# Attention's block-end visits two steps later, with their pieces on four PSUM tiles, and the sorting of tokens spread into single steps

## The chip, the cores and the metric

One core of one Trainium2 chip. The metric is the device time of one execution in microseconds (us), 1326.75 at the median of three runs of the kernel before. Engines are named as the profile names them: PE (TensorE), DVE (VectorE), ACT (ScalarE), POOL (GpSimd), SP (SyncE, which here issues most DMAs).

## The reference

The input is `x` of shape (2, 256, 56, 56): B = 2 images, C = 256 channels, N = 56·56 = 3136 tokens each. Cut to what is computed:

```
h   = non-local conv block(x)                 # gram matrices, 1x1 convs, batch norm, residual
t   = layernorm(tokens of h)                  # (2, 3136, 256)
t   = t + causal_attention(t, 4 heads of 64) @ W_proj
u   = layernorm(t)
p   = softmax(u @ W_gate)                     # 8 experts
top-2 experts per token, with their weights
t   = t + sum over its 2 experts of  w_e * (gelu(u @ W1[e] + b1[e]) @ W2[e] + b2[e])
out = t as (2, 256, 56, 56)
```

## The kernel before

**Stages.** The conv block takes the first 100 us or so. Attention goes to about 867 us, and the experts from there to the end. Within attention, token work of other kinds is fed in: the projections of the next stretch of tokens, the output projection of blocks that are finished, and the sorting of tokens by expert.

**Attention** (`attend`, L684 on). For each image b, each query block i of W = 448 tokens (7 of them) and each head pair hp (2) the kernel goes over the key tiles j of 128 tokens. All steps (i, hp, j) are written out into one list. A step has two halves. `scores` makes the products of keys and queries (L721) in a PSUM tile with the tag "sc" (two buffers), ACT takes their exponential (L729), DVE masks the tiles that the diagonal cuts (L731) and adds the rows up in `acc` (L739, L743). `values(n - 3)`, three steps later, multiplies with the values (L761) into the PSUM tile yp, of which there is one. After the last key tile ACT copies yp (L772) to `both`, and POOL adds its halves into `qT` (L773).

**Block ends.** When the scores of a block's last key tile are written, `visit(i, hp)` (L1966) and `sum_rows` (L776) follow on the spot. A visit runs the pieces that `ahead` (L1928) names: projections to query and key (qk, L603), to value (v, L618) or transposes (xp, L589) of the next stretch of tokens; two steps of the queue (`pull`); and two steps of the output projection (`products`, pp, L671). A piece makes some matmuls in a PSUM tile that `bank` (L522) gives from a pool of two, and ACT (L595, L611, L627) or DVE (L676) empties it. `sum_rows` sums `acc` over partitions (sp, L785); the sums go through DRAM (L790 to L796), `invert` (L805) takes the reciprocal, it goes out and comes back broadcast (L806, L811), and `scale` (L817) applies it to the block.

**The queue.** `tokens(b)` is a generator in a queue: `project_out` (L671: products, DVE sum, the statistics of the layernorm at L177 and L178), then `dispatch` (L1004: reciprocal root by Newton steps at L1040 to L1053, softmax, top 2, ranks by expert), then the scatter of token rows into expert order (`x_slots`, L1355 to L1363: DVE makes a row tile xr, POOL issues two indirect DMAs for each of 25 chunks of 128 tokens), and for b = 0 the loads of W1 (w1s, L1845) and of the experts' first rows. Each `yield` ends a step. `pull(n)` takes n steps. `between` (L1977), called once in every step of attention, pulls two steps at every second call.

**Experts** (L1380 to L1661). Some 102 blocks of 128 rows: the hidden layer ht (L1485), gelu (L1494), the transposes of a later block's inputs (tp, L1462), a copy of a later block's weights by DVE (w_f, L1473), the output yp (L1504), its bias (ys, L1514) and its store (y_slots, L1519, on SP). Blocks 0 to 41 are image 0's. Image 1's queue goes on beside them: `meanwhile` pulls two steps a block, three while image 1 is being sorted. The rows come in groups of three blocks. Group 14 (blocks 42 on) is the first with rows of image 1; it is fetched (L1403) at block 36, and ahead of that `need(1)` pulls the queue until all scatters of image 1 are issued. When the group has landed, DVE tests it (eq, L1428), adds two parts of its mixed rows (L1439), and goes on to the weights of block 41. A check of the softmax sums, `judge` (L1784 to L1789), ends in a small matmul, gdp (L1793).

**What sets the order.** In attention and in the experts the order on every engine is the order in which the program is written (`manual_schedule`), so the lists, the yields and the pulls above decide where an instruction stands on its engine.

Of the kernel before, what the change touches and what calls it, by code (L numbers as in the profile page):

```python
# [10 lines left out]
F32 = mybir.dt.float32  # L11
# [17 lines left out]
def conv_attn_moe_kernel(  # L29
# [52 lines left out]
    P = 128  # L82
# [429 lines left out]
    def layer1(nm, general):  # L512

        with ExitStack() as whole:
# [4 lines left out]
            bg = pool(whole, "bg", bufs=2)  # L519
            g1 = pool(whole, "g1", bufs=1)  # L520

            def bank(name, shape=(P, 512)):  # L522
                return pm.tile(list(shape), F32, tag="m", name=f"{name}_{nm}")

            def centre_gate(place):
# [135 lines left out]
            def project_out(b, qT, done):  # L661

                for first, m, k in pairs():
                    while done() < (first + m - 1) * P + k:
                        yield False
                    yield "pe"
                    for n in range(first, first + m):
                        o = n * P
                        ps = bank(f"pp_{b}_{n}")
                        for c in range(NH):  # L670
                            nc.tensor.matmul(  # L671
                                ps[:k, : C + E], qT[:, c, o : o + k], wpr[:, c, :],
                                start=(c == 0), stop=(c == NH - 1),
                            )
                        t = ts[b][:k, n, : C + E]
                        nc.vector.tensor_tensor(t, t, ps[:k, : C + E], ALU.add)  # L676
                        if b == 0:
                            nc.sync.dma_start(out=rest_d[:k, n], in_=t[:, :C])
                    stats(b, first, m, k, bg, f"o{nm}{b}")

                    for _ in range(3 if b else 1):
                        yield True

            def attend(  # L684
                b, qT, kT, v, fst, fs, psc, py, visit, between, clock, later, finished
# [62 lines left out]
                def values(n):  # L748
                    i, hp, j, first, last, order = steps[n]
                    k = chunk(j)  # L750
                    c0 = max(0, j * P - i * W)
                    sn = f"{nm}{b}_{hp}_{i}"
                    st = sts.pop(n)
                    if first:
                        yps[hp, i] = py.tile([P, 2, 512], F32, tag="y", name=f"yp_{sn}")
                    yp = yps[hp, i]

                    for h in range(0, k, HS):
                        end = last or (h and all(chunk(o) <= h for o in order[order.index(j) + 1 :]))
                        for a in range(2):  # L760
                            nc.tensor.matmul(  # L761
                                yp[a * HS : (a + 1) * HS, h // HS, c0:W],
                                v[hp][h : h + HS, j, a, :HS],
                                st[h : h + HS, a, c0:],
                                start=first,
                                stop=bool(end),
                            )
                    if last:

                        yh = qT[:, hp, i * W : (i + 1) * W]  # L770
                        both = fs.tile([P, 2, W], F32, tag="acc", name=f"both_{sn}")
                        nc.scalar.copy(both, yp[:, :, :W])  # L772
                        nc.gpsimd.tensor_tensor(yh, both[:, 0], both[:, 1], ALU.add)  # L773
                        del yps[hp, i]

                def sum_rows(hp, i):  # L776
                    yh = qT[:, hp, i * W : (i + 1) * W]
                    r = (b * NH + hp) * NB + i
                    sn = f"{nm}{b}_{hp}_{i}"
                    acc = accs.pop((hp, i))  # L780
                    sp = bank(f"sp_{b}_{hp}_{i}")

                    flat = acc.rearrange("p a w -> p (a w)")
                    for g in range(4):
                        nc.tensor.matmul(  # L785
                            sp[g * 32 : (g + 1) * 32, : W // 2], ones[:, :32],
                            flat[:, g * W // 2 : (g + 1) * W // 2], start=True, stop=True,
                        )
                    line = fs.tile([P, W], F32, tag="rb", bufs=3, name=f"line_{sn}")
                    nc.scalar.copy(line[:, : W // 2], sp[:, : W // 2])  # L790
                    halves = sum_d[r].rearrange("a (h w) -> (a h) w", h=2)
                    for g in range(4):
                        nc.sync.dma_start(
                            out=halves[g : g + 1], in_=line[g * 32 : g * 32 + 1, : W // 2]
                        )
                    nc.sync.dma_start(  # L796
                        out=sums[:, r], in_=sum_d[r].rearrange("a (p f) -> (a p) f", p=HS)
                    )
                    later.append((clock[0] + 4, invert, hp, i, yh))
# [27 lines left out]
                        later.sort(key=lambda e: e[0])  # L827

                ends = {i: max(n for n, s in enumerate(steps) if s[0] == i) for i in range(NB)}
                LAG = 3  # L830
                for n in range(len(steps) + LAG):
                    if 0 < n <= len(steps) and steps[n - 1][4]:
                        i, hp = steps[n - 1][:2]
                        visit(i, hp)
                        sum_rows(hp, i)
                    if n < len(steps):
                        i = steps[n][0]
                        between(i, ends[i] - n)

                    late = n >= LAG and steps[n - LAG][3]  # L840
                    if n >= LAG:
                        due(clock[0])
                        clock[0] += 1
                    if n >= LAG and not late:
                        values(n - LAG)
                    if n < len(steps):
                        scores(n)
                    if late:
                        values(n - LAG)
# [154 lines left out]
            def dispatch(b):  # L1004

                t = ts[b]
                tail = chunk(NCH - 1)
                ops = [0]

                def small_piece():  # L1010

                    if b:
                        yield True
# [5 lines left out]

                def op():  # L1020

                    ops[0] += 1
                    for _ in range(0 if b else 1 + ops[0] % 2):
                        yield True

                def small(name, last=E, dt=F32):
# [2 lines left out]
                def wide(ap):  # L1029
# [8 lines left out]
                    small(k, 1).rearrange("p t o -> p (t o)") for k in ("newton_x", "newton_y", "red")  # L1038
                )
                nc.vector.tensor_scalar(x, var, 1e-5, None, ALU.add)  # L1040
                nc.vector.tensor_scalar(
                    y.bitcast(I32), x.bitcast(I32), 1, None, ALU.arith_shift_right
                )
                nc.vector.tensor_scalar(
                    y.bitcast(I32), y.bitcast(I32), -1.0, float(0x5F3759DF), ALU.mult, ALU.add
                )
                yield from small_piece()
                for i in range(4):
                    to = var if i == 3 else y
                    nc.vector.tensor_tensor(z, y, y, ALU.mult)  # L1050
                    nc.vector.tensor_tensor(z, z, x, ALU.mult)
                    nc.vector.tensor_scalar(z, z, -0.5, 1.5, ALU.mult, ALU.add)
                    nc.vector.tensor_tensor(to, y, z, ALU.mult)  # L1053
                    yield from op()
                    yield from small_piece()
# [294 lines left out]
                for n in range(NCH):  # L1350
# [23 lines left out]
                        if b or k:  # L1374
                            yield True
                    if b == 0:
                        yield False
                sent[b] = True

            def experts(w1s, w2s, b2s, ex, es, ps6, between, need, written, settle, decide):  # L1380
# [538 lines left out]
            else:  # L1919
                fst = pool(att, "fst", bufs=5)  # L1920
                fs = pool(end, "fs", bufs=2, side="right")
                psc = pool(att, "psc", bufs=2, space=PSUM)
                py = pool(att, "py", bufs=1, space=PSUM)
                projections = [project_qkv(b, qT, kT, v, px) for b in range(B)]
                finished = [[0] * NH for b in range(B)]
# [37 lines left out]
                for b in range(B):  # L1963
                    queue.append(tokens(b, qT, lambda b=b: min(finished[b])))

                    def visit(i, hp):  # L1966

                        now, then = ahead(b, i, hp)
                        for piece in now:
                            piece()  # L1970
                        for _ in range(2):
                            pull()
                            products()
                        for piece in then:
                            piece()

                    def between(i, left):  # L1977
                        if b == B - 1 and i == NB - 1:

                            now = load_w2(left < NCH - 4)  # L1980
                            for _ in range(1 if left > NCH - 4 else 2):
                                next(now, None)

                        tick[0] += 1
                        if tick[0] % 2:
                            pull(2)

                    due = attend(
                        b, qT, kT, v, fst, fs, psc, py, visit, between,
# [252 lines left out]
```

## Time and profile before

| | us |
|---|---|
| runs | 1324.08, 1326.75, 1327.43 |
| the profiled execution | 1320.51 |
| its span, first to last instruction | 1318.7 |
| PE busy (96% of the span) | 1269.1 |
| DVE busy (61%) | 798.3 |
| ACT busy (46%) | 610.9 |
| POOL busy (26%) | 348.8 |
| a full step of attention (L721 and L761) | 1.50 |
| a block of the experts | 3.73 |
| scatters of image 1 on POOL | 958.66 to 1035.81 |

The mean granted clock of PE is 0.991. A row of the timeline reads: start, duration, engine, line, operation, output <- inputs, shapes, count, and in brackets the idle time of the engine just ahead of it with what ended it. In the view of waits a row names the instruction that waited, what it waited for, the sum in us, how often, and the longest. "issue" is time in which an engine waited for nothing that the profile shows.

### The profile page before, as it was taken

How to read it: one execution, taken by the hardware profiler on the slowest of the kernel's cores; microseconds unless marked ns; L12 is line 12 of the kernel's file. 1: busy time of each engine (PE TensorE's matmuls, PEld its weight loads, DVE VectorE, ACT ScalarE, POOL GpSimd, SP SyncE). 2: the span in 40 equal slices, each digit the busy share in tenths (PEclk: the TensorE clock that was granted, in tenths of full speed). 3: DMA queues.
4: the chain of work that ended last, by engine and by line, in shares of the span. 5: the costliest groups of instructions: out<-in, count | busy, mean ns of one | idle time of the engine just before them, and what ended most of it. 6: DMA issues, size and time to landing. Idle time of an engine off the chain costs nothing.

```text
span 1318.7 us, 28564 instructions
## 1 busy us (share of the span) xinstructions
PE 1269.1 (96%) x10809; PEld 827.2 (63%) x10809; DVE 798.3 (61%) x1673; ACT 610.9 (46%) x1235; POOL 348.8 (26%) x319
## 2 busy tenths in 40 slices
PE   9999999999999999999999999999998999899997
PEld 8875445544444555444444444579987899799996
DVE  1673566666777745756877777754753443355554
ACT  0255555556566544555655455633432333344432
POOL 1113330000002223311126620000066312665551
PEclk9999999999999999999999999999999899999999
DMA  9994100000000001000002243321234343466654
GB/s 317 359 349 129 31 16 24 25 17 16 17 9 8 25 1 37 18 11 9 16 24 81 81 133 95 105 72 53 69 128 147 117 113 94 139 195 193 189 162 132
DMA packets 111074, 123.88 MB, mean 94 GB/s; under 512 B 19703, under 2 KB 100840, under 8 KB 110930
## 3 DMA queue, kind: packets, MB, share of 16 engines
q1 hardware_dynamic: 100130, 95.18, 23.7%
q0 software_dynamic: 9840, 25.67, 5.7%
q8 instruction: 89, 1.46, 0.5%
q10 hardware_dynamic: 960, 1.11, 0.3%
q14 instruction: 55, 0.45, 0.1%
HBM read 62.06 MB, written 61.05 MB: 93 GB/s over the span
## 4 chain that ended last, share of the span: by engine, by line
PE 87%; DVE 6%; ACT 3%; issue 3%; DMA 1%; POOL 0%; SPq 0%; DVEq 0%; ACTq 0%; POOLq 0%
PE sc_f L721 18%; PE yp_f L761 18%; PE ht_f L1485 14%; PE yp_f L1504 13%; PE qk_f L603 7%; PE v_f L618 3%; PE cp L410 3%; DVE acc_f L743 2%; PE gram L317 2%; PE pp_f L671 2%; ACT st_f L729 2%; PE tp_f L1462 2%; PE sp_f L785 1%; PE yo_f L1727 1%; DMA out_dram<-ot_f 1%
## 5 line engine op out<-in xcount | busy, mean ns | idle before, releaser
L729 ACT ACTIVATE st_f<-sc_f 128x896 f32<-128x896 f32 (+5 forms) x400 | 330.4, 840 | 225.0 <-PE sc_f L721 199.3
L743 DVE TENSOR_TENSOR acc_f<-acc_f,st_f 128x896 f32<-128x896 f32 (+5 forms) x372 | 379.9, 1021 | 74.0 <-ACT st_f L729 62.2
L721 PE MATMUL sc_f<-qT_f,kT_f 64*64 64x448 f32 (+6 forms) x3184 | 340.6, 500 | 9.4 <-ACT st_f L729 6.0
L761 PE MATMUL yp_f<-st_f,v_f 64*64 64x448 f32 (+6 forms) x3184 | 339.9, 501 | 3.5 <-DVE st_f L731 2.3
L1494 ACT ACTIVATE g_f<-ht_f,b1b 128x128 f32<-128x128 f32 x408 | 116.5, 370 | 252.0 <-PE ht_f L1485 125.1
L721 PEld LDWEIGHTS sc_f<-qT_f,kT_f 64*64 64x64 f32 x3184 | 121.0, 133 | 164.5 <-issue 124.2
L761 PEld LDWEIGHTS yp_f<-st_f,v_f 64*64 64x64 f32 x3184 | 120.0, 133 | 154.3 <-issue 131.7
L1485 PE MATMUL ht_f<-xT_f,w_f 128*128 128x128 f32 x1632 | 206.4, 280 | 4.5 <-issue 3.6
L1485 PEld LDWEIGHTS ht_f<-xT_f,w_f 128*128 128x128 f32 x1632 | 201.7, 196 | 11.3 <-issue 6.0
L773 POOL TENSOR_TENSOR qT_f<-both_f 128x448 f32<-128x448 f32 x28 | 37.0, 1321 | 503.0 <-ACT both_f L772 503.0
L1363 POOL DMA_INDIRECT x_slots<-xr_f,idx x100 | 110.0, 1100 | 144.0 <-DVE xr_f L1361 100.8
L1473 DVE COPY w_f<-w1s_f 128x1024 f32 x102 | 72.7, 714 | 84.8 <-PE ht_f L1485 37.7
L574 POOL TENSOR_SCALAR xn_f<-t 128x256 f32<-128x256 f32 (+1 forms) x50 | 80.8, 1624 | 155.3 <-PE xp_f L589 66.2
L1525 POOL DMA_INDIRECT y_tokens<-ys_f,to_f x57 | 59.0, 1036 | 126.1 <-DVE ys_f L1514 102.3
L1514 DVE TENSOR_TENSOR ys_f<-yp_f,kT_f 128x128 f32<-128x128 f32 x102 | 29.5, 289 | 102.8 <-PE yp_f L1504 72.8
L603 PE MATMUL qk_f<-px_f,wat 128*128 128x512 f32 (+2 forms) x224 | 88.5, 547 | 0.8 <-ACT px_f L595 0.6
L603 PEld LDWEIGHTS qk_f<-px_f,wat 128*128 128x128 f32 x224 | 40.5, 190 | 46.2 <-issue 41.1
L739 DVE COPY acc_f<-st_f 128x896 f32<-128x896 f32 x28 | 17.9, 641 | 80.1 <-ACT st_f L729 76.3
L1504 PE MATMUL yp_f<-v_f,g_f 128*128 x204 | 62.2, 385 | 2.0 <-issue 1.9
L731 DVE TENSOR_TENSOR st_f<-st_f,keep 128x256 f32<-128x256 f32 (+1 forms) x112 | 45.6, 407 | 30.4 <-ACT st_f L729 29.8
L1504 PE MATMUL yp_f<-px_f,g_f 128*128 x204 | 62.3, 385 | 1.4 <-issue 1.4
L1504 PE MATMUL yp_f<-kT_f,g_f 128*128 x204 | 61.9, 384 | 1.1 <-issue 1.0
(285 smaller groups left out, 1268.4 us busy)
## 6 DMA issues: line engine op xcount, KB each, us to landing
x_slots<-fill SPq DMA_DIRECT2D x1, 8190.0 KB
xb_f<-x_slots SPq DMA_DIRECT2D x60, 130.0 KB
x_slots<-fill SPq DMA_DIRECT2D x1, 7296.0 KB
y_slots<-ys_f SPq DMA_DIRECT2D x57, 128.0 KB
kept<-t SPq DMA_DIRECT2D x2, 3200.0 KB
x<-in_x_dram SPq DMA_DIRECT2D x14, 448.0 KB
rb_f<-inverses SPq DMA_DIRECT2D x56, 112.0 KB
y_f<-y_tokens SPq DMA_DIRECT2D x23, 256.0 KB
```

Source lines behind the costliest of these rows:

```text
L574: nc.gpsimd.tensor_scalar(xn[:k, a], ts[b][:k, n + a, :C], ts[b][:k, n + a, MEAN : MEAN + 1], ts[b][:k, n + a, RSTD : RSTD + 1], ALU.subtr ...
L603: nc.tensor.matmul(ps[:, :w], wat[:, c, d0 : d0 + P], px[:, s % 2, c, :w], start=(c == 0), stop=(c == NH - 1),)
L721: nc.tensor.matmul(ps[h : h + HS, a, c0:W], kT[hp][rows, j * P + h : j * P + h + HS], qT[rows, hp, q0 + c0 : q0 + W], start=True, stop=True,)
L729: nc.scalar.activation(st[:k, :, c0:], ps[:k, :, c0:W], AF.Exp, scale=SCALE)
L743: nc.vector.tensor_tensor(acc[:k, :, c0:], acc[:k, :, c0:], st[:k, :, c0:], ALU.add)
L761: nc.tensor.matmul(yp[a * HS : (a + 1) * HS, h // HS, c0:W], v[hp][h : h + HS, j, a, :HS], st[h : h + HS, a, c0:], start=first, stop=bool( ...
L1363: s = nc.gpsimd.indirect_dma_start(out=xds[b], out_offset=bass.IndirectOffsetOnAxis(ap=idxs[b][:kk, k, n : n + 1], axis=0), in_=xr[:kk], i ...
L1473: nc.vector.tensor_copy(w, w1s[:, :, bass.ds(e, 1), :].rearrange("p c e h -> p c (e h)"))
L1485: nc.tensor.matmul(ht[:, k, :], w[:, c, k * P : (k + 1) * P], xT[:, c, :], start=(c == 0), stop=(c == NH - 1),)
L1494: nc.scalar.activation(g[:, k, :], ht[:, k, :], AF.Gelu, bias=b1bs[b][:, k, i : i + 1])
L1504: nc.tensor.matmul(yp[:, :C], g[:, k, :], w2s[k][:, bass.ds(e, 1), :].rearrange("p e d -> p (e d)"), start=(k == 0), stop=(k == KH - 1),)
L1525: s = nc.gpsimd.indirect_dma_start(out=y_tokens, out_offset=bass.IndirectOffsetOnAxis(ap=to[:, n % GB : n % GB + 1], axis=0), in_=ys, in_o ...
```

## The change

It has these parts. (1) A visit comes when the scores of two steps of the next block are written (`BEHIND = 2`), and `sum_rows` with it. (2) In a visit the pieces take in turn two tiles of the pool "m" and two of the scores' pool (`ring`). (3) `both` no longer has a buffer of its own and uses `acc`'s. (4) For image 0 the statistics after the output projection become a later piece per chunk (`closer`), put at the head of the queue, and three yields follow for either image. (5) In image 0's dispatch each operation, Newton's too, is a step of one yield; one yield was no step (`False`) behind its scatter and becomes one. (6) Visits pull no longer; `between` pulls one step at each call, but for the cut tiles of block 0. (7) W2's loads in the last block start a little later.

```diff
             def bank(name, shape=(P, 512)):
+                turn = ring[0] % 4 if ring else 0
+                if turn > 1:
+                    ring[0] += 1
+                    flat = score_banks[0].tile([P, 2, 512], F32, tag="sc", name=f"{name}_{nm}")[:, 0]
...
+                    return flat[:, : shape[1]]
+                if ring:
+                    ring[0] += 1
                 return pm.tile(list(shape), F32, tag="m", name=f"{name}_{nm}")
...
+                    if b == 0:
+                        queue.appendleft(closer(b, first, m, k))
+                        continue
                     stats(b, first, m, k, bg, f"o{nm}{b}")
 
-                    for _ in range(3 if b else 1):
+                    for _ in range(3):
                         yield True
+                while b == 0 and unclosed[0]:
+                    yield False
+
+            unclosed = [NCH]
+
+            def closer(b, first, m, k):
+
+                for n in range(first, first + m):
+                    stats(b, n, 1, k, bg, f"o{nm}{b}")
+                    unclosed[0] -= 1
+                    yield True
...
-                        both = fs.tile([P, 2, W], F32, tag="acc", name=f"both_{sn}")
+                        both = accs.pop((hp, i))
...
-                    acc = accs.pop((hp, i))
+                    acc = accs[hp, i]
...
-                LAG = 3
+                LAG, BEHIND = 3, 2
                 for n in range(len(steps) + LAG):
-                    if 0 < n <= len(steps) and steps[n - 1][4]:
-                        i, hp = steps[n - 1][:2]
+                    if BEHIND < n <= len(steps) + BEHIND and steps[n - 1 - BEHIND][4]:
+                        i, hp = steps[n - 1 - BEHIND][:2]
                         visit(i, hp)
                         sum_rows(hp, i)
                     if n < len(steps):
                         i = steps[n][0]
-                        between(i, ends[i] - n)
+                        between(i, ends[i] - n, (steps[n][2] + 1) * P > i * W + 1)
...
-                    ops[0] += 1
-                    for _ in range(0 if b else 1 + ops[0] % 2):
+                    if b == 0:
                         yield True
...
                     if b == 0:
-                        yield False
+                        yield True
                 sent[b] = True
...
                         now, then = ahead(b, i, hp)
+                        ring.append(0)
                         for piece in now:
                             piece()
                         for _ in range(2):
-                            pull()
                             products()
                         for piece in then:
                             piece()
-
-                    def between(i, left):
-                        if b == B - 1 and i == NB - 1:
+                        ring.clear()
+
+                    def between(i, left, cut):
+                        if b == B - 1 and i == NB - 1 and left < NH * NCH - 2:
...
                         tick[0] += 1
-                        if tick[0] % 2:
-                            pull(2)
+                        if not cut or i:
+                            pull()
```

In the order of the built programs, the rows of PE are the same in kind and number. The visits stand two steps later; the scatters of image 0 end 10 to 14 steps later; the output projection of image 1 has six chunks more behind attention; its ranks, keys and scatters stand five blocks of the experts later (its first row tile behind w_27, before behind w_22). At block 36, nine chunks of the scatter are left where there were two. From block 41 on the orders are the same.

## The prediction

> **What bounds the kernel now.** I read the busy shares first, then the costliest groups, then what TensorE (PE) waits for, and only then the stretches of time in which it waits.
>
> ```profile
> span 1318.7 us, 28564 instructions
> PE 1269.1 (96%) x10809; PEld 827.2 (63%) x10809; DVE 798.3 (61%) x1673; ACT 610.9 (46%) x1235; POOL 348.8 (26%) x319
> L721 PE MATMUL sc_f<-qT_f,kT_f 64*64 64x448 f32 (+6 forms) x3184 | 340.6, 500 | 9.4 <-ACT st_f L729 6.0
> ```
>
> PE is busy 96% of the span, so only 1318.7 - 1269.1 = 49.6 us are to be had at all without fewer matmuls. The order of instructions in the two programs shows the same 7387 rows on PE, so the change removes no matmul: it can only remove idle time of PE or add some. The view of what PE waits for says what the idle time is:
>
> ```profile
> PE sc_f L721 <- ACT st_f L729: 6.0, 9, 1.2
> PE yp_f L1504 <- issue: 4.2, 7, 1.0
> PE ht_f L1485 <- issue: 3.6, 8, 1.1
> ...
> PE gdp_f L1793 <- DVE judge_f L1789: 2.3, 1, 2.3
> PE yp_f L761 <- DVE st_f L731: 2.3, 4, 1.0
> PE xp_f L589 <- DVE t L676: 2.2, 6, 1.1
> ...
> PE sp_f L785 <- ACT kT_f L611: 1.8, 7, 0.3
> PE sp_f L785 <- DVE t L676: 1.1, 2, 0.6
> ```
>
> (us in total, times, longest.) Waits of the visits (xp L589, sp L785, qk, pp) are many and small. The timeline of one visit shows their form:
>
> ```profile
> 286.67 5.43 PE L603 MATMUL qk_f<-px_f,wat 128*128 128x384 f32 x16
> 291.93 3.72 PE L671 MATMUL pp_f<-wpr,qT_f 128*128 128x264 f32 x16
> 295.88 0.41 PE L589 MATMUL xp_f<-ident,xn_f 128*128 128x128 f32 x2 [0.23 <-DVE t L676]
> 296.22 0.58 PE L785 MATMUL sp_f<-acc_f,ones 128*32 128x224 f32 x8
> ```
>
> A visit of 10 us loses 0.23 us here. So the visits are long but full, and the second half of the profile, where the stall per occurrence is microseconds, weighs as much as they do.
>
> **Part 1: visits later, pieces on four tiles.** No instruction is added. Each gap of PE of 0.16 us or more between 104 and 866 us sums to about 19 us; by kind: sp, thirteen of 0.17 to 0.35 us, 3.2; xp 2.2 (one alone 1.15); pp 0.6; qk 0.2. These 6.2 us are waits for one of two tiles to be emptied, and four tiles give two more pieces (about 1.8 us by the pp row, 0.93 us each) of cover, so I count them gone. The two sp waits of 0.57 at 824.84 and 863.30 us come in the last block's visits, where few pieces rotate: they stay. Of the other gaps, yp<-DVE mask L731 (2.3 us, in four places) ends when two further steps of scores lie between a mask and its use: 0 to 2.3. The scatter zone of batch 0 (698 to 771 us: sc<-ACT exp 4.9, issue 2.0) sees its scatters spread over more steps and 10 to 14 steps later: 0 to 3. Against it: yp of the next block waits for ACT's copy L772 where the block is short (0.45 us in two places now, rows of i=0): with a visit's evacuations in ACT's queue ahead of the exps, 0 to 0.9 more. What hides the later sum chain (sums DMA, invert, inverses DMA, rb DMA: 3.8 + 4.2 + 3.7 us) is the next block, tens of us; its cover is gone only at the last block. Sum: -4 to -11 us, taken -7.5, near the 6.2 whose rows are plain plus something of the rest.
>
> A rule that speaks against it: the Trainium skill, "TensorE: Matmul & The Clock Gate", section "A second HAM failure mode: psum-queue depth-cycling", says that cycling through PSUM banks can leave micro-gaps that make the clock drop and recover over and over. The window rows here grant 1.00 in every stretch of attention while two tiles already turn; so by the row it costs nothing, by the rule the visits would run partly at half clock. I take the row.
>
> **Part 2: the end of attention.** At the change to the experts, sums go 864.3 to 870.4, inverses to 874.9, rb to 879.1, and DVE stands behind that chain: PE waits 1.48 us for a pp tile at 880.29 and 0.78 at 867.02. The last visit now comes after more of the closing values (L761), so the chain begins about 1.1 us later against the end of attention, and fewer pieces (pp of batch 1, six tiles of 0.89 = 5.3 us) remain done before it; that is work moved, not added. Cost 0 to +2.5, taken +1.5.
>
> **Part 3: batch 1's sorting comes later.** Visits no longer pull the queue, variances are pieces of their own, and every sorting step waits a turn. In the instruction order of the changed program the rank of batch 1 moves from before block 18 of the experts to before block 23, its first scatter row from after w_22 to after w_27: five blocks, at 3.73 us a block 18.7 us. The scatters must all be issued before the load of group 14, which the order puts at block 36 in both programs. Before, 2 chunks of 25 are left there; after, 9 (16 to 24), written in a row between w_37 and w_38. POOL's rows price them:
>
> ```profile
> 1038.55 0.19 PE L1793 MATMUL gdp_f<-ones,judge_f 128*1 128x1 f32 x2 [2.33 <-DVE judge_f L1789]
> 1038.66 3.44 PE L1485 MATMUL ht_f<-xT_f,w_f 128*128 128x128 f32 x16
> ...
> 1051.60 1.95 PE L1485 MATMUL ht_f<-xT_f,w_f 128*128 128x128 f32 x16
> ```
>
> ```profile
> 958.66 0.99 POOL L1363 DMA_INDIRECT x_slots<-xr_f,idx  x1 [90.54 <-DVE xr_f L1361]
> ...
> 989.49 0.97 POOL L1363 DMA_INDIRECT x_slots<-xr_f,idx  x1 [0.30 <-issue]
> ```
>
> One scatter is 0.97 + 0.30 us, a chunk two of them, 2.56; 25 chunks cannot take less than 64 us, and took 77.15 (958.66 to 1035.81). Now let S be 958.66. Before, block 36 starts at S + 69.7, POOL ends at S + 77.2, group 14 is issued on SP at 1037.51, lands and meets its test on DVE (eq L1428) at 1044.74 without a wait, and block 41 (ht at 1051.60) is S + 92.9: the load has several us to spare. After, the scatters start near block 27, S + 18.7. Nine more blocks at the rate that blocks 22 to 36 had under scatters (68.8 us for 14, 4.92 each) put block 36 at S + 63. Then 9 x 2.56 = 23 us, and some 2.6 us that POOL is behind by then (one chunk): POOL ends at S + 88.6. Then 1.7 us to SP's issue, 6 to the landing, 0.5 for eq and to, 0.96 for the sum L1439, 0.69 for the copy w_41 L1473, which stands behind them on DVE: block 41 starts near S + 98.4. Behind SP's waiting load stand y_slots of blocks 33 to 35, whose buffers (three) DVE needs again at block 36's rows; that stands behind w_41 too and ends with the same landing. So block 41 comes 5 us later. PE, done with block 40 at S + 82, stands idle some 14 us there; the stalls of 14.7 us "issue" that it has under scatters now (969 to 974, 999 to 1003, 1016 to 1021 us) are fewer, which is already in the 5.
>
> The clock adds to it. After 2.33 us of idle the row at 1038.66 shows 3.44 us for the 16 matmuls that take 1.95 in the row at 1051.60, and the window 1020 to 1040 a clock of 0.84. A longer idle should cost some 2.5 us (one slow ht, 1.5, and the slow yp behind it). The Trainium skill, the same page, "What's actually happening", gives half rate after an idle window of about 3.4 us and full rate after as long a busy one; by that the price would be about 1.7 us, as an estimate, and our 2.33 us of idle would not always be enough, while the row shows that it was.
>
> Bounds: if POOL has nothing left over and half of the 14.7 us of stalls go, block 41 is no later than now (0); if none of them go and they fall beside the burst, +14. Taken +7.5 (5 and 2.5).
>
> A gain I exclude: nothing is taken from PE or POOL in this part, and even at POOL's floor the scatters end at S + 18.7 + 64 = S + 82.7, after the S + 77.2 of before.
>
> **Spaced sorting of batch 0** (Newton steps one by one, the second scatter as a step): DVE does the same work, in more places. Its cover is attention; it ends about 14 steps (some 20 us) later, still before block (1,0,6), and the first rows for the experts are loaded behind it; w1s (8 loads) go beside w2's on SP. They still come 60 us ahead of the experts, so nothing. If that cover were gone: the first block would wait for the loads of early rows, some 6 us by the landing above.
>
> **Sum.** -7.5 + 1.5 + 7.5 = +1.5 us against the profiled execution, 1320.51 us (span 1318.7 and 1.8 around it): 1322.0. The median of the runs shown, 1326.75, lies 6.2 above it (their spread is 1324.08 to 1327.43), so I predict 1328.3.
>
> **Rivals.**
> - As forecast, gain and loss cancel: 1325 to 1331. Chance 0.36.
> - Faster: attention gives all (-9 to -11), and the wait at block 41 is hidden, since the stalls under scatters that go are as long as it (0 to +2): 1317 to 1322. For it: 14.7 us of such stalls exist. Against: the burst is written in the order, and POOL's rate has no slack in its rows. Chance 0.28.
> - Slower: the burst of nine chunks alone sets the time of block 41, and none of the stalls under scatters pay for it. It decides once POOL ends more than 13 us after block 36 starts (now 7.5; by my working 25). Its price is the upper bound, +12 to +14, with attention's and the turn's terms as above: -7.5 + 1.5 + 13 = +7 on 1326.75, so 1334, and 1331 to 1338 with the spread of attention's term. For it: POOL's rows have no slack in them, and the load has no second way. Chance 0.34.
> - It does not do what it says: visits wait as before, now for exps of the two steps ahead (sc tiles are shared with the scores). Then the 6.2 us stay, and the loss stays too: near 1335. Chance 0.02, and it counts with slower.
>
> A measurement of this kernel tells about 0.3%, 4 us, from no change. From these cases: faster 0.28, same 0.36, slower 0.36. The range, which leaves about 0.1 out at each end: 1317 to 1337.
>
> **What would show it.** In the profile after: the waits of xp, sp and qk in visits down to about 1 us together; the first scatter of batch 1 some 13 us after that of before (18.7, less what is gained ahead of it), nine chunks back to back on POOL, ending over 20 us after the start of block 36; DVE's eq L1428 with a wait for the xb DMA of some 10 us, and an idle stretch of PE of 10 us or more before block 41 with a clock of 0.8 or less in that window. I am wrong if that stretch is not there (then faster), or if the waits of the visits are (then slower).

## The result, and the profile after

The changed kernel takes 1330.74 us at the median of 13 runs (1326.35 to 1337.03), the kernel before 1326.28 in as many beside it: a ratio of 1.0044, 95% interval 1.0029 to 1.0058. That is slower by some 0.4%, just over the 0.3% that the prediction called no change, and inside its range. The profiled execution took 1329.87 us against 1320.51, 9.4 more; the medians differ by 4.5, since the profiled execution of before lies under all 13 of its runs. So the losses in the table below, read off these two profiles, are some 5 us larger in sum than those of the medians.

The page of the changed kernel, and what PE waits for (us in total, times, longest):

```profile
span 1328.2 us, 28525 instructions
PE 1268.9 (96%) x10809; PEld 824.0 (62%) x10809; DVE 785.1 (59%) x1673; ACT 612.8 (46%) x1235; POOL 345.9 (26%) x319
```

```profile
PE ht_f L1514 <- issue: 12.9, 19, 1.6
PE yp_f L1533 <- issue: 10.6, 11, 2.2
PE sc_f L746 <- ACT st_f L754: 5.1, 7, 1.9
...
PE sp_f L810 <- DVE t L687: 0.6, 1, 0.6
...
PE gdp_f L1822 <- DVE judge_f L1818: 0.5, 1, 0.5
```

The waits of the visits have nearly gone, as forecast: xp is no longer in the list, qk keeps its 0.6 us, and sp 1.6 us of its 4.4 (2.2 us together, where about 1 was forecast). What has grown is "issue" in the experts, from 7.8 to 23.5 us on ht and yp. The same visit as was shown of before, in the timeline:

```profile
284.19 5.43 PE L614 MATMUL qk_f<-px_f,wat 128*128 128x384 f32 x16
289.45 3.72 PE L682 MATMUL pp_f<-wpr,qT_f 128*128 128x264 f32 x16
293.01 0.38 PE L600 MATMUL xp_f<-ident,xn_f 128*128 128x128 f32 x2
293.32 0.59 PE L810 MATMUL sp_f<-acc_f,ones 128*32 128x224 f32 x8
```

From the first pp to sp it takes 3.87 us where it took 4.29. The bracket of before showed 0.23 us of idle there, but 0.42 us went: the row of pp is 3.72 long, and the next instruction can start 3.56 after it began. A bracket begins at the modelled end of the row before it, so the wait here is some 0.16 us longer than it says.

Where the time went, by the starts of the experts' blocks (us from the span's start, read off the ht rows of both timelines):

| | before | after | after less before |
|---|---|---|---|
| block 21 (the projections moved out of attention are done) | 955.8 | 942.2 | -13.6 |
| block 36 (group 14 is fetched) | 1028.3 | 1009.9 | -18.4 |
| block 41 (needs group 14 on DVE's way) | 1051.6 | 1057.1 | +5.5 |
| end of the span | 1318.7 | 1328.2 | +9.5 |

At block 21 the ranks of image 1 (about 1 us of PE) are done in before and still to come in after, so some 12.6 of the 13.6 us are gain. So attention gave about twice what was forecast, five blocks took back 23.9 us, and the rest 4.0; of these 2.3 are in waits of yo for DVE (3.3 us, before 1.0), and what the others are is not shown. In the five blocks PE did not stand at block 41, as the prediction had it. It crawled. The timeline, PE, then POOL at the same time:

```profile
1022.36 0.56 PE L1514 MATMUL ht_f<-xT_f,w_f 128*128 128x128 f32 x1 [0.38 <-issue]
1024.50 0.37 PE L1514 MATMUL ht_f<-xT_f,w_f 128*128 128x128 f32 x1 [1.57 <-issue]
1025.93 0.37 PE L1514 MATMUL ht_f<-xT_f,w_f 128*128 128x128 f32 x1 [1.06 <-issue]
...
1043.74 0.19 PE L1822 MATMUL gdp_f<-ones,judge_f 128*1 128x1 f32 x2 [0.54 <-DVE judge_f L1818]
1043.86 3.78 PE L1514 MATMUL ht_f<-xT_f,w_f 128*128 128x128 f32 x16
```

```profile
1036.99 0.91 POOL L1392 DMA_INDIRECT x_slots<-xr_f,idx  x1 [0.30 <-issue]
1038.21 0.91 POOL L1392 DMA_INDIRECT x_slots<-xr_f,idx  x1 [0.30 <-issue]
```

One matmul, at times two or three, in 0.7 to 2.8 us, from 1014 us on, for as long as POOL issues the scatters of the burst without a break, and some 4 us more. Block 37 takes 30.1 us. In before there are three such stretches, of 4 to 5 us (from 969, 999 and 1015 us). Behind the crawl one block is slow (block 38, 5.7 us), then PE goes at its full rate, and the rows of group 14 are not waited for: DVE tests them as soon as it has done what stands ahead of the test (no bracket), and blocks 40 and 41 start 3.73 us apart.

```profile
1050.21 0.15 DVE L1457 TENSOR_TENSOR eq_f<-xb_f,sid 128x3 f32<-128x3 f32 x1
```

### The profile page after: what moved, and what is told of

Its sections match the earlier page's. It is cut to its first block, busy times and chain, and to the rows that moved or that the text cites. A ratio compares the mean times of both kernels' runs of the same rounds, so it can differ in the third digit from the quotient of the medians.

```text
span 1328.2 us, 28525 instructions
## 1 busy us (share of the span) xinstructions
PE 1268.9 (96%) x10809; PEld 824.0 (62%) x10809; DVE 785.1 (59%) x1673; ACT 612.8 (46%) x1235; POOL 345.9 (26%) x319
## 4 chain that ended last, share of the span: by engine, by line
PE 91%; issue 2%; DVE 2%; ACT 2%; another core or an unknown queue 1%; DMA 1%; POOL 0%; DVEq 0%; SPq 0%; ACTq 0%; POOLq 0%
PE yp_f L786 20%; PE sc_f L746 19%; PE ht_f L1514 14%; PE yp_f L1533 13%; PE qk_f L614 7%; PE v_f L629 4%; PE cp L410 3%; PE pp_f L682 3%; PE gram L317 2%; PE tp_f L1491 2%; PE sp_f L810 1%; PE yo_f L1756 1%; ACT st_f L754 1%; PE xp_f L600 1%
## 5 line engine op out<-in xcount | busy, mean ns | idle before, releaser
L768 DVE TENSOR_TENSOR acc_f<-acc_f,st_f 128x896 f32<-128x896 f32 (+5 forms) x372 | 374.6, 1007 | 149.8 <-ACT st_f L754 132.9
L746 PE MATMUL sc_f<-qT_f,kT_f 64*64 64x448 f32 (+6 forms) x3184 | 337.1, 500 | 7.5 <-ACT st_f L754 5.1
L786 PE MATMUL yp_f<-st_f,v_f 64*64 64x448 f32 (+6 forms) x3184 | 339.6, 502 | 4.0 <-ACT acc_f L797 2.0
L1514 PE MATMUL ht_f<-xT_f,w_f 128*128 128x128 f32 x1632 | 208.3, 280 | 16.0 <-issue 12.9
L786 PEld LDWEIGHTS yp_f<-st_f,v_f 64*64 64x64 f32 x3184 | 117.1, 133 | 158.2 <-issue 128.7
L798 POOL TENSOR_TENSOR qT_f<-acc_f 128x448 f32<-128x448 f32 x28 | 31.9, 1138 | 467.2 <-ACT acc_f L797 467.2
L585 POOL TENSOR_SCALAR xn_f<-t 128x256 f32<-128x256 f32 (+1 forms) x50 | 84.8, 1704 | 157.0 <-PE xp_f L600 68.6
L1533 PE MATMUL yp_f<-w2s_f,g_f 128*128 x204 | 62.2, 386 | 2.1 <-issue 2.0
L756 DVE TENSOR_TENSOR st_f<-st_f,keep 128x256 f32<-128x256 f32 (+1 forms) x112 | 45.1, 403 | 29.2 <-ACT st_f L754 28.2
```

Of the source, the lines that this page charges most:

```text
L585: nc.gpsimd.tensor_scalar(xn[:k, a], ts[b][:k, n + a, :C], ts[b][:k, n + a, MEAN : MEAN + 1], ts[b][:k, n + a, RSTD : RSTD + 1], ALU.subtr ...
L746: nc.tensor.matmul(ps[h : h + HS, a, c0:W], kT[hp][rows, j * P + h : j * P + h + HS], qT[rows, hp, q0 + c0 : q0 + W], start=True, stop=True,)
L768: nc.vector.tensor_tensor(acc[:k, :, c0:], acc[:k, :, c0:], st[:k, :, c0:], ALU.add)
L786: nc.tensor.matmul(yp[a * HS : (a + 1) * HS, h // HS, c0:W], v[hp][h : h + HS, j, a, :HS], st[h : h + HS, a, c0:], start=first, stop=bool( ...
L1514: nc.tensor.matmul(ht[:, k, :], w[:, c, k * P : (k + 1) * P], xT[:, c, :], start=(c == 0), stop=(c == NH - 1),)
L1533: nc.tensor.matmul(yp[:, :C], g[:, k, :], w2s[k][:, bass.ds(e, 1), :].rearrange("p e d -> p (e d)"), start=(k == 0), stop=(k == KH - 1),)
```

## The experiments

All of them ran where the kernel before takes 1286 us and not 1326 (on chips 10, 4, 3 and 2 by the record; that of the first comparison is not on it); so each is compared, by the ratio, with runs of the kernel before made beside it. In attention, the kernel before of the first comparison and before_late_sort, whose attention has no edit, agree within 0.3 us up to 680 us. In the view of waits of eleven of these twelve runs PE has no line marked "issue"; only early_after_chain has one, of 2.7 us, and that one ends as the mixed rows of group 14 are ready.

Positions in image 1's sorting are by blocks of the experts. Theory A: a long unbroken run of scatters on POOL slows PE. Theory B: the burst delays group 14, and block 41 waits for it (the prediction's).

**early_dense.**

```diff
-                    pull(3 if sorting or worked[0] >= MIXED else 2, every=True)
+                    pull(3 if not projected[1] else 3 if sorting or worked[0] >= MIXED else 2, every=True)
```

> The changed kernel with one edit: beside the experts, three steps of the queue are pulled per block (not two) until image 1 is projected. In the order of instructions image 1's first scatter then stands behind block 20 (27 in the changed kernel), 1.5 chunks a block follow, and none of a burst is left for block 36. Theory A (PE gets its instructions slowly while POOL issues scatters back to back for longer than some 10 us; the burst of nine chunks cost 24 us of PE at blocks 37 and 38): the burst's 24 us go, the short stalls of the before kernel come back in part, so 15 to 22 us less than the changed kernel, 1308 to 1316. Theory B, the rival of the prediction (the burst only delays the load of group 14, and PE would have been slow for another reason, such as the weights copy behind the row tiles on DVE): 5 to 8 us less than the changed kernel, and PE is still slow around block 37.

Measured: 1270.9 us, ratio 0.9883 (0.9867 to 0.9900), 15.1 us below the kernel before. Against the changed kernel, run again below, it is some 20 us less: in the range of theory A and not of B, but without what theory A speaks of, since PE shows no wait for issue here at all; POOL ends its scatters at 997.7 us, just after block 37 begins (995.7), and block 41 is not waited for.

**early_paced.**

```diff
-                    pull(3 if sorting or worked[0] >= MIXED else 2, every=True)
+                    pull(6 if not sent[1] and not placed[1] else 2 if not sent[1] else 3 if worked[0] >= MIXED else 2, every=True)
```

> The changed kernel with one edit: six steps of the queue per block until image 1's places are known, and two (one chunk, two scatters) per block while it is scattered; by the order of instructions one chunk a block from block 10 to block 35, so POOL is busy with scatters 2.56 us of every 3.73. Theory A (long unbroken runs of scatters starve PE): no run is longer than one chunk, so the stalls marked issue between blocks 10 and 41 fall from over 20 us to under 4, and the time is 5 to 12 us below early_dense, 1298 to 1308. Rival (PE stalls with any scatter, by their number): the same sum of stalls as early_dense, spread over more blocks, and the same time within 4 us.

Measured: 1285.38 us, ratio 0.9993 (0.9983 to 1.0003). Both expectations missed. Its two longest waits of PE:

```profile
PE rank_f L1151 <- DVE both_f L1140: 7.2, 1, 7.2
PE pp_f L682 <- DVE t L687: 6.6, 1, 6.6
```

Pulled too fast, the queue puts PE work (the last projections, the ranks) in PE's order before DVE can have fed it. The first pp waits while the row-sum chain of the last block is still under way (sums, inverses, rb): DVE stands until 847.79 us for the landing of rb, and PE with it. The rank waits because DVE is at work on what the ranks are made from (Newton steps, softmax, top 2, from 884 to 898 us).

**before_late_sort.**

```diff
-                    pull(3 if sorting or worked[0] >= MIXED else 2, every=True)
+                    pull(0 if 4 <= worked[0] < 9 else 3 if sorting or worked[0] >= MIXED else 2, every=True)
```

> The kernel before with one edit: the queue is not pulled in five blocks of the experts (4 to 8), so that image 1's sorting comes five blocks later and nine to ten chunks are left for block 36, as in the changed kernel, while attention is untouched. Theory A: the burst starves PE here too: +15 to +22 us on the before kernel, 1341 to 1348, with PE's rows of one or two matmuls some 0.7 to 2 us apart behind block 36. Theory B (the loss comes with something else in the change): +5 to +8 us, and only as a wait of block 41 for its rows.

Measured: 1305.06 us, ratio 1.0154 (1.0132 to 1.0176), +19 us: theory A's number with theory B's picture. One line of the view of waits holds all of it:

```profile
PE tp_f L1462 <- DVE xb_f L1439: 18.7, 1, 18.7
```

PE goes at 3.7 to 4.0 us a block from block 36 to block 40 and stands there for the mixed rows of group 14. Later sorting alone, without anything else of the change, makes this loss.

**burst_with_gaps.**

```diff
                     while not sent[b]:
                         pull(every=True)
+                        if b:
+                            for _ in range(2):
+                                nc.gpsimd.memset(fill[:, :C], 0.0)
```

> The changed kernel, where each scatter of the burst at block 36 is followed by two POOL memsets of a zero tile that stays zero (128 x 256), so that the scatters of the burst are further apart. Theory A (the unbroken run starves PE): PE goes through blocks 37 to 40 at close to 3.73 us, and then stands at block 41 until the group's load has landed, some 10 us after POOL's end; the time within 8 us of the changed kernel. Rival (the number of scatters outstanding, not their spacing, starves it): PE is as slow at blocks 37 and 38 as in the changed kernel, and for longer, +10 to +20 us.

Measured: 1303.51 us, ratio 1.0134 (1.0117 to 1.0151), some 12 us over the changed kernel below. PE does what was expected, blocks 37 to 40 in 3.8 us each and then a wait behind xb, but the time is 4 us beyond the bound given.

```profile
PE tp_f L1491 <- DVE xb_f L1468: 32.6, 1, 32.6
```

The last scatter ends 12.9 us later than in changed_again (1031.9 for 1019.0) and block 41 starts 12.7 us later (1043.9 for 1031.2): block 41 follows POOL's end one to one.

**changed_again.** No edit.

> The changed kernel itself, unedited, beside the kernel before on the chip of these runs. In the last four runs no wait of PE was marked issue, and the kernel before took 1286 us where it took 1326 in the first comparison. Theory C (two prices for the same burst): where PE is not short of instructions, it reaches block 41 early and waits there for its rows, as forecast; attention gives some 15 us and the wait takes 15 to 22, so 1284 to 1294 if before is at 1286, with one wait of PE behind the sum of the mixed rows (xb) of 14 to 20 us. Theory D (the loss of the first comparison was the short supply of instructions alone): no such wait, and 1268 to 1274, as early_dense. If this chip shows the waits marked issue again: near 1330, with them at blocks 37 and 38.

Measured: 1291.5 us, ratio 1.0035 (1.0022 to 1.0047). Theory C holds, its wait at the upper bound. Its waits, the rows of PE around the longest, those of DVE in it, and POOL's last scatter:

```profile
PE tp_f L1491 <- DVE xb_f L1468: 20.2, 1, 20.2
```

```profile
1005.16 1.95 PE L1514 MATMUL ht_f<-xT_f,w_f 128*128 128x128 f32 x16
1027.32 0.66 PE L1491 MATMUL tp_f<-ident,xb_f 128*128 128x128 f32 x2 [20.21 <-DVE xb_f L1468]
1027.77 1.06 PE L1533 MATMUL yp_f<-px_f,g_f 128*128 x2
...
1031.18 2.64 PE L1514 MATMUL ht_f<-xT_f,w_f 128*128 128x128 f32 x16
...
1035.61 1.95 PE L1514 MATMUL ht_f<-xT_f,w_f 128*128 128x128 f32 x16
```

```profile
1024.06 0.16 DVE L1457 TENSOR_TENSOR eq_f<-xb_f,sid 128x3 f32<-128x3 f32 x1 [21.95 <-DMA xb_f<-x_slots]
...
1026.26 0.96 DVE L1468 TENSOR_TENSOR xb_f<-xb_f,xo_f 128x768 f32<-128x768 f32 x1 [1.63 <-DMA xo_f<-x_slots]
1027.13 0.69 DVE L1502 COPY w_f<-w1s_f 128x1024 f32 x1
```

```profile
1018.07 0.91 POOL L1392 DMA_INDIRECT x_slots<-xr_f,idx  x1 [0.30 <-issue]
```

This is the forecast's chain, but for two links: POOL ends at 1019.0, SP issues the load 1.7 us later (1020.68), DVE's test comes 3.4 us after that (the forecast had 6 to the landing), the mixed rows land 1.6 us behind it, and the sum follows. PE stands not for the weights copy but for this sum, at the transposes tp (1027.32); the yp rows of block 40 come next, and block 41 starts 3.9 us behind tp, at 1031.2: the forecast had block 40 done by then. The clock, too, is as it said: after the idle stretch yp runs at 1.06 for 0.59 and block 41's ht at 2.64 for 1.95 us.

**dense_visits_at_end, dense_two_tiles, dense_neither.** All on early_dense: `LAG, BEHIND = 3, 0`; the line `ring.append(0)` taken out; both.

```diff
-                LAG, BEHIND = 3, 2
+                LAG, BEHIND = 3, 0
...
-                        ring.append(0)
```

> early_dense with BEHIND = 0: visits and row sums at a block's end as before, all else of the change left in (four tiles, spread steps). If the later visits carry the gain of attention: 8 to 12 us over early_dense; if the four tiles carry it: within 3 us of it. The waits of xp and sp come back in the first case.

> early_dense with the pieces on two tiles as before, the visits still two steps later. If the four tiles carry the gain: 8 to 12 us over early_dense, with the waits of sp for ACT's copies back; if the later visits carry it: within 3 us.

> early_dense with visits at the block's end and pieces on two tiles; what is left of the change is the spreading of the sorting and of the variances. If visits and tiles together carry all of attention's gain (15 us): 13 to 16 us over early_dense; if the spreading carries a half of it: 6 to 9 us.

Measured: 1276.51 us, 0.9922 (0.9895 to 0.9948); 1277.62, 0.9932 (0.9914 to 0.9951); 1284.39, 0.9983 (0.9973 to 0.9993). Against early_dense (0.9883) that is +5, +6 and +13 us: both parts carry about as much, and they add up. The first two expectations gave either part all or nothing, and missed. The third falls at the edge of its first branch, though a third of attention's gain is left without either part; both its branches took that gain to be 15 us, and it is nearer 19 (24.0 less the 5.3 below). The rows of ACT that copy a finished yp (28 in attention) place it; differences to before_late_sort in us:

| block finished | early_dense | visits at end | two tiles | neither |
|---|---|---|---|---|
| image 0, last | -5.5 | -4.2 | -2.5 | -0.3 |
| image 1, block 3 | -13.0 | -10.1 | -8.0 | -4.3 |
| image 1, last | -24.0 | -17.9 | -17.6 | -11.3 |

The last row holds 5.3 us of projections that moved to the experts. Without either part, 11.3 - 5.3 = 6 us remain at the end: what the rest of the change gave, the spread steps and the visits that no longer pull (nearly all in image 1, where the statistics and sorting of image 0 lie). None of that was tried alone.

**before_early.** The kernel before with early_dense's edit.

> The kernel before with the one edit of early_dense (three steps of the queue per block until image 1 is projected): its scatters start behind block 17 in place of 22 and end before block 36. If the early sorting pays only where attention's gain has pulled the experts ahead of their rows: within 4 us of the kernel before, where PE shows no waits marked issue. Rival (earlier sorting is a gain of its own, and early_dense owes it half of its 15 us): 6 to 8 us under it. Where PE does show waits marked issue, the scatters are as many and as dense, so the same, within 5 us.

Measured: 1293.81 us, ratio 1.0056 (1.0039 to 1.0073), slower by 7 to 8 us; both expectations missed. The reason is that of early_paced, two waits that before_late_sort, whose sorting is later, has not (pp 0.6 us, rank none):

```profile
PE pp_f L671 <- DVE t L676: 6.9, 2, 6.3
...
PE rank_f L1122 <- DVE both_f L1111: 2.4, 1, 2.4
```

So earlier sorting is no gain of its own. It paid where the rows would have been late; that the changed kernel's six more chunks of projections, which cover the row-sum chain, also had a part in it is likely, but was not tried alone.

**early_dense_again and early_four.** The second has 4 in place of early_dense's first 3.

> early_dense again. Where the kernel before is at 1286: 0.988 of it, as the first time. Where the kernel before is at 1326 (PE short of instructions beside scatters): if the loss of the first comparison was the burst, attention's gain of some 13 us stays and the short stalls stay as they are: 0.987 to 0.992 of it.

> As early_dense with four steps per block until image 1 is projected: scatters start behind block 17, and end by block 33. If the rows are no longer waited for in early_dense, no further gain: within 3 us of it. If DVE's earlier work delays PE, as in early_paced (waits of pp and rank for DVE, 6.6 and 7.2 us): 3 to 8 us over it.

Measured: 1269.81 us, 0.9873 (0.9857 to 0.9890), as the first time; and 1277.14, 0.9926 (0.9909 to 0.9943), 6 to 7 us over it, the second branch: pp waits 4.6 us and rank 2.0.

**early_after_chain.**

```diff
-                    pull(3 if sorting or worked[0] >= MIXED else 2, every=True)
+                    pull(2 if worked[0] < 1 else 3 if not projected[1] else 3 if sorting or worked[0] >= MIXED else 2, every=True)
```

> The changed kernel with three steps of the queue per block until image 1 is projected, as early_dense, but two per block while no block's output is done (about the first three blocks), so that the last row-sum chain can end first. In the order of instructions image 1's scatters start behind block 22 and two chunks are left for block 36, as in the kernel before. If the wait of pp for DVE (2.9 us in early_dense_again) is all that early_dense paid for pulling early: that wait falls under 1 us and the time is 1 to 3 us under early_dense, 0.984 to 0.987 of the kernel before. Rival (two chunks left at block 36 are already late here, since PE comes to block 36 earlier than in the kernel before): a wait behind the mixed rows (xb) of 1 to 6 us, and 0.988 to 0.992.

Measured: 1272.48 us, 0.9889 (0.9873 to 0.9906). The wait of pp has gone, but block 41 starts 8.3 us after block 40 (1013.33, 1005.06) and not 3.7: the rival. Its wait is the one marked "issue": tp starts at 1009.74, 0.1 us after DVE's sum of the mixed rows ends. With two chunks left at block 36 the rows are late already, by 4.5 us, because the experts start earlier. early_dense stays the lowest of the kernels run, though the intervals do not part it from this one.

## Why the prediction was right, and where it was not

**The sum was near, its terms were not.** Forecast -7.5 + 1.5 + 7.5 = +1.5; measured about +5.8 by the ratio (4.5 by the medians). Attention and the turn together were forecast at -6 and gave -13.6 (block 21, first comparison) and -15.7 (block 20 of changed_again, 926.8, against 942.5 in before_late_sort). The expert stage was forecast at +7.5 and took 23.9 from block 36 to 41 and 4.0 behind it, less 4.8 gained before, so 23.1. Each was wrong by a factor of two to three, in opposite directions; that the sum came near is luck. Within the first, the turn (the change from attention to the experts) costs 2.5 us in changed_again (by ACT's last yp row 18.2 gained at attention's end, the 5.3 moved taken off, and 15.7 left at block 20) where 1.5 was forecast, above all a wait of 2.3 us of block 0's ht for its weights copy.

**Attention: the term was mis-sized.** The step that failed is "These 6.2 us are waits for one of two tiles to be emptied ... I count them gone". They are gone, but they were not all. First, brackets leave out a part: they begin at modelled ends, 0.16 us late in the visit above. Counted from the start of a PE row to the start of the next, pp and xp together take 48.5 us in dense_two_tiles and 42.1 in early_dense, so 6.4 us went with the tiles alone. With the later visits the scores' and values' rows themselves are shorter: 335.8 and 337.3 us busy in the page of burst_with_gaps where before_late_sort has 340.7 and 340.5, and so in all eight of the twelve runs that have later visits (335.8 to 335.9, 337.3 to 337.4), beside 339.9 and 339.5 to 339.6 in dense_visits_at_end and dense_neither. Why a row is shorter is not shown. Second, the rest of the change gave 6 us where "0 to 3" stood. The sum of bracketed idle time between 100 us and the first ht of the experts fell from 15.0 to 7.9 us (before_late_sort, burst_with_gaps), which is what the prediction would have measured; the gain is twice that.

**The rule against four tiles** was weighed rightly: every window of 100 us from 100 to 700 us has a granted clock of 1.00 in the changed kernel too, and that from 700 to 800 (image 0's scatters) 0.98 in the first comparison and 1.00 in changed_again.

**Sorting later: the chain was right, its price was mis-sized.** The first scatter comes 5.6 us after that of before and not 13, which is five blocks less the larger gain (18.7 - 13.6 = 5.1). From the start of block 36 to POOL's end the prediction had 25.6 us; it is 29.2 in both profiles of the changed kernel, for the most part since 11 chunks were still to be issued and not ten. From POOL's end to block 41 it had 9.8; changed_again shows 12.2: the landing came 2.6 us sooner than its 6, but it had put at nothing the 1.6 us wait on the mixed rows and the 3.9 us of tp and yp that PE still had to run. And it let block 36 come 6.7 us earlier (S + 63 for S + 69.7), since five more blocks would run without stalls under scatters. In the first comparison blocks 21 to 36 gave 4.8 us back, 5.8 without the ranks; where there are no such stalls, as in changed_again, nothing could come back.

**What the prediction did not have** is the way in which PE lost the time in the first comparison. It said that PE stands at block 41 for some 14 us, and that it is wrong, then faster, if that stretch is not there. The stretch is not there in the first comparison, and the kernel was not faster: PE crawled through block 37 for 30 us instead, and the crawl, not the rows, set the start of block 41. Block 41 then came 17.9 us after POOL's end, where the chain took 12.2 in changed_again. So the crawl cost an estimated 5.7 us beyond the wait that would have stood there anyway: a crawl and a wait under the same cover cost the longer of the two. Theory B is shown where PE does not crawl (before_late_sort, burst_with_gaps, changed_again). Theory A's run length is not: in before_late_sort and changed_again POOL issues all 50 scatters of image 1 without a break of 1 us, where the longest run of the first comparison is 26, and PE keeps 3.7 to 4.0 us a block from block 36 on until its wait. What slows PE in the first comparison stays open; it came up in none of the twelve runs, so nothing could be tried on it. That PE, ACT (25.9 us, "issue") and DVE (15.7) stood at once, beside unbroken scatters, is all that the trace tells.

**The clock** after the idle stretch was forecast at 2.5 us. In changed_again the rows from tp (1027.32) to the start of block 42 (1035.61) take 8.3 us where they take 5.7 at full rate: 2.6, after 20.2 us of idle. The same stretch costs 1.9 us in before_late_sort (18.7 of idle), 2.4 in burst_with_gaps (32.6) and 1.6 in early_after_chain (2.7), so the price did not grow with the idle time, and that changed_again comes so near to 2.5 is chance. The Trainium skill, "TensorE: Matmul & The Clock Gate", section "What's actually happening", would have given 1.7 us as an estimate, which is nearer to two of the four. That 2.33 us of idle is enough, as the prediction read off one row, holds in some executions only: block 0's ht follows a wait of 2.33 us in nine profiles and takes 2.02 us in six of them, 2.53, 2.73 and 3.49 in the others.

**Rivals.** The slower one has the mechanism of changed_again: POOL ended 29.2 us after block 36 began, where 13 was the turning point, and its expert term (12 to 14) was closer than the forecast's, though still too small. In the first comparison the crawl stood in its place, and the time, 1330.74, lies where "as forecast" ends (1331) and the slower one begins. The faster one is, by its ratio, what early_dense makes of the change, 0.988, but by early sorting and not by stalls that went.

## What to carry to other kernels

A queue that is fed between other work has a due time at its far end: before work is taken out of it, count from the order of instructions how many of its steps are left when the first reader comes, and price them at the slowest engine's rate. Idle time in brackets can be too small where ends of rows are modelled; compare the starts of two rows across the place. And a change that gains early and loses late should be tried with the late loss alone mended: here one number in one line turned +0.4% into -1.2%, while the same line alone made the kernel before 0.6% slower.

## What the runs showed of the hardware

The same program lost its time in two ways: 20.2 us in one wait at block 41 (granted clock 0.68 in the 20 us that follow 1020), or as 27 us in which PE issued one matmul, at times two or three, in 0.7 to 2.8 us beside back-to-back indirect DMAs (0.50):

```profile
1000.00:1020.00 20.00, 7.10 (x50) 6.52 (x48) 0.86 (x3) 3.62 (x14) 14.71 (x15) 0.80 0.29 100
1020.00:1040.00 20.00, 12.68 (x68) 11.59 (x69) 7.07 (x20) 3.17 (x11) 0.00 (x0) 0.68 0.48 133
```

```profile
1000.00:1020.00 20.00, 16.73 (x104) 14.44 (x102) 10.64 (x42) 4.20 (x15) 13.10 (x14) 0.93 0.35 122
1020.00:1040.00 20.00, 5.76 (x13) 3.52 (x13) 0.69 (x1) 1.51 (x5) 14.85 (x15) 0.50 0.29 100
```

The first two lines are changed_again, the others the first profile of the changed kernel; the columns are PE, PEld, DVE, ACT and POOL busy, the granted clock, the DMA share and GB/s. The ratio to the kernel before is nearly the same in both, 1.0035 and 1.0044, but not for one cause: in changed_again the chain from POOL's last scatter sets the start of block 41, in the first comparison the crawl does.
